# Layer-norm graph attention on one core: the last four batches' projections in plain float32, and another order for the end

## The chip, the core and the metric

The kernel runs on one core of a Trainium2 chip. The metric is the device time in microseconds. Before the change three runs took 1846.33, 1846.67 and 1848.8 us, so the median is 1846.67 us. One more run was taken with a profile; it took 1845.31 us, of which 1843.2 us lie between the first and the last instruction (the span). All times inside the kernel below come from that profiled execution.

The engines are named as in the profile: PE is the matrix engine (PEld its weight loads), DVE the vector engine, ACT the scalar engine, POOL the general engine, SP the engine that issues most DMAs.

## What is computed

The input `x` is 128 batches of 128 x 512 float32, `adj` one 128 x 128 matrix for all. Two layers, cut to what matters:

```python
# layer 0: W = adj, r = relu(rowmax(W @ x) + b)
x = layernorm(x + r)
# layer 1: masked attention with 8 heads of 64, then a projection, a norm, a residual
q, k, v = split(x @ w_qkv)                       # 512 -> 3 x 512
attn = softmax(where(adj == 0, -inf, q @ k.T / 8))
o = (attn @ v) @ w_proj + b_proj                 # 512 -> 512, the projection
o = o + layernorm(o) * gamma + beta
x = layernorm(x + o)
```

## The kernel before, in words

**Split products.** Every dense product (q, k, v and the projection) is made from a high part, a low part and a difference of each operand, in a float32 type that the matrix engine takes in a single pass (`fp32r` in the rows). `product` (L809) makes 8 matmuls of 128 x 512 into one bank of the accumulator memory and `product_d` (L816) makes 4 more into another. The two are joined when they are read. For the projection of batch b the left operand is made as follows after the attention product `AV` (L938): `omask` (L959) cuts off the low bits on DVE, `osub` (L962) makes the rest on DVE, `ohigh` (L965) scales the high part on ACT (on POOL for every fourth batch), and `od` (L968) subtracts on POOL. Then come `po` (8 matmuls), `pod` (4 matmuls), `pmain` (L1005, DVE: first bank plus bias) and `prest` (L1017, DVE: adds the second bank and sums the row). The three forms of `w_proj` are made once, at the start, and stay in place.

**Plain float32 products.** A matmul of plain float32 operands appears in the profile as two matmul records. The kernel before uses such products in five places: `conv` (L626), two v products at the very start (L773), the scores `S` (L847), `AV`, and the transposes.

**Stages of a batch.** Load, row maximum (`conv`, `cmax`), the first norm (`norm0`), a transpose of `x` by DMA (`xpl`, `xrow`, `xcross`), its split forms (`xmask`, `xsub`, `xhigh`, `xd`), the dense products of a group of four batches (`dm`, `dd`, read by `main` on ACT and `rest` on DVE), `S`, `masked`, `rmax`, `exps`, `recip`, `wts` (the softmax), the transpose of the weights by DMA (`pln`, `row`, `cross`), `AV`, the projection, and then the tail: `sq1`, `sm1`, `st1`, `n1a`, `n1b` (norm of o, scaled, and added to the residual), `sq2`, `sm2`, `st2`, `norm2` (the last norm), `out`. `res`, `resx`, `resb`, `reso` reload `x`, renew its norm, add beta, and add o; `resx`, `resb` run on POOL, `reso` on POOL for the first batch of the last group and on DVE for the other three.

The weights of the last group (batches 124 to 127) are transposed on PE (`T`, `wT`) and not by DMA.

**What sets the order.** A batch is b = 4g + i, in groups g of four, g = 0 to 31. Each step has a place: a planner's time in the tables `FIRST`, `STEADY`, `LAST`, plus 55.2952 for each group. `plan.sort` (L1149) sorts all steps by place and emits them in this order, so each engine runs its own instructions in the order of the places. Only the order counts; the numbers themselves are no times in the last two groups (`LAST[-2]` for 120 to 123, `LAST[-1]` for 124 to 127). `TWO` chooses the engine or form of single steps; `HOMES` says, for each kind of tile and each group, which of a few buffers it uses. A step whose buffer is still being read waits for that reader.

**What exists but is not used.** `plain`, `lp`, `ocopy` (L974 to L987), and the first branches of `po` and `pmain` are already in the code. `TWO["plain"]` is all zero and the tables have no `lp` or `ocopy`, so none of them is issued.

Of the kernel before, what the change touches and what calls it, by code (L numbers as in the profile page):

```python
# [8 lines left out]
FP = mybir.dt.float32  # L9
# [60 lines left out]
    'pmain': [83.702, 69.241, 100.828, 106.975],  # L70
# [13 lines left out]
    'norm2': [110.625, 102.524, 149.986, 131.962],  # L84
# [119 lines left out]
        'load': [-91.734, -89.477, -107.242, -114.634],  # L204
        'conv': [-79.525, -78.308, -102.395, -106.644],
        'cmax': [-78.282, -74.809, -97.173, -102.720],
        'relu': [-74.462, None, -95.620],
        'bn': [-84.588, -84.468],
        'ba': [-79.682, -83.743],
        'rstdx': [-78.667],  # L210
        'shiftx': [-73.931],
        'add0': [None, None, -94.016, -93.757],
        'sq0': [None, None, -92.245, -92.088],
        'rstd0': [None, None, -90.665],
        'shift0': [None, None, 1.956],
        'norm0': [-72.634, -70.162, -87.160, -65.629],
        'xpl': [-70.704, -62.494, -82.728, -52.644],
        'xrow': [-67.509, -55.672, -79.256, -47.934],
        'xcross': [-61.696, -54.959, -69.654, -44.141],
        'xmask': [-56.802, -49.006, -67.480, -38.547],  # L220
        'xsub': [-56.208, -47.336, -48.300, -38.074],
        'xhigh': [-56.405, -35.357, -48.848, -36.590],
        'xd': [-13.227, -33.711, -14.237, -9.757],
        'dm': [21.746, 35.982, 28.529, 24.986, -12.154, -20.919, -31.752, -22.843, -16.374, -23.208, 3.153, -23.262],
        'dd': [23.983, 44.501, 28.964, 43.094, -0.464, -0.154, -2.296, 3.849, 2.837, 6.978, 9.141, -3.429],
        'main': [25.819, 57.797, 40.607, 32.331, -7.607, -8.068, -28.601, -21.948, -7.441, -14.251, 7.551, -22.713],
        'rest': [26.194, 59.179, 55.083, 48.674, 1.465, 1.877, 5.828, 8.803, 4.926, 9.286, 9.980, -0.010],
        'S': [12.874, 24.637, 13.908, 27.284],
        'masked': [15.703, 26.864, 16.095, 31.214],
        'rmax': [15.733, 40.798, 24.980, 58.564],  # L230
        'exps': [19.267, 49.838, 29.967, 74.789],
        'recip': [20.091, 53.481, 40.286, 110.599],
        'wts': [21.502, 58.271, 41.826, 298.180],
        'pln': [29.804, 61.505, 44.952, 425.772],
        'row': [29.811, 62.249, 56.821, 855.336],
        'cross': [71.356, 71.129, 392.061, 855.704],
        'AV': [450.591, 228.845, 746.233, 898.316],
        'omask': [674.319, 308.605, 1366.729, 1365.220],
        'osub': [770.925, 364.572, 1435.526, 1878.235],
        'ohigh': [754.357, 413.868, 1441.862, 1849.429],  # L240
        'od': [988.972, 501.318, 1621.330, 2107.197],
        'po': [974.369, 651.327, 1588.162, 2528.823],
        'pod': [1064.642, 652.548, 1865.274, 2557.810],
        'pmain': [1435.941, 736.245, 1973.007, 2868.655],
        'prest': [1546.675, 797.306, 2173.489, 2884.326],
        'res': [74.125, 210.960, 1968.966, 1160.560],
        'resx': [666.741, 389.233, 2173.124, 1523.596],
        'resb': [1621.095, 663.168, 2352.412, 1829.810],
        'reso': [1640.878, 1001.671, 2395.120, 2960.734],
        'sq1': [1604.545, 997.678, 2512.030, 2977.847],  # L250
        'sm1': [1686.157, 999.741, 2175.055, 3079.791],
        'st1': [1828.719, 1108.345, 2545.132, 3018.165],
        'n1a': [1812.470, 1044.747, 2812.405, 3131.435],
        'n1b': [1850.820, 1165.266, 2862.346, 3159.644],
        'sq2': [2493.237, 1760.632, 2976.836, 3254.808],
        'sm2': [1921.825, 1828.948, 3018.160, 3473.653],
        'st2': [2528.768, 2033.360, 3135.653, 3542.995],
        'norm2': [2639.507, 2052.978, 3248.824, 3833.127],
        'out': [2968.875, 2348.409, 3425.425, 3981.636],
    },  # L260
    -1: {
        'load': [-74.411, -94.944, -121.973, -105.338],
        'conv': [-67.640, -67.401, -118.263, -97.835],
        'cmax': [-66.723, -65.650, -114.893, -95.280],
        'relu': [-58.744, None, -89.292],
        'bn': [-61.917, -72.350],
        'ba': [-60.526, -67.833],
        'rstdx': [-56.851],
        'shiftx': [-56.726],
        'add0': [None, None, -62.987, -77.999],  # L270
        'sq0': [None, None, -57.978, -56.682],
        'rstd0': [None, None, -53.335],
        'shift0': [None, None, -44.091],
        'norm0': [-51.929, -48.752, -41.363, -43.244],
        'xpl': [-47.768, -35.477, -40.163, -26.662],
        'xrow': [-47.424, -34.373, -36.605, -25.909],
        'xcross': [-44.093, -25.037, -30.491, -19.630],
        'xmask': [-35.420, -9.955, -16.920, -10.187],
        'xsub': [-25.027, -6.256, -12.316, -6.545],
        'xhigh': [-27.780, -5.984, -14.077, -6.723],  # L280
        'xd': [-3.120, 2.338, -1.405, 2.029],
        'dm': [313.202, 1288.056, 1009.352, 606.354, 5.041, -3.508, 3.931, -0.002, 5.901, 0.270, 3.338, 5.883],
        'dd': [1260.174, 1334.786, 1944.004, 2066.246, 15.556, 181.181, 16.195, 16.891, 14.449, 10.199, 16.353, 204.999],
        'main': [531.917, 1726.881, 2232.003, 1492.821, 19.146, 4.178, 12.068, 2.946, 20.970, 15.386, 13.588, 251.078],
        'rest': [1584.380, 2117.448, 2732.560, 2262.970, 213.729, 258.245, 214.247, 228.661, 100.506, 20.060, 216.387, 259.031],
        'S': [390.580, 829.031, 841.642, 913.116],
        'masked': [618.393, 1107.535, 1243.436],
        'rmax': [666.560, 1118.244, 1747.034, 1340.778],
        'exps': [953.376, 1201.075, 2054.184, 1674.549],
        'recip': [2062.103, 1344.889, 2203.646, 1765.129],  # L290
        'wts': [2152.417, 1549.500, 2396.365, 2203.399],
        'T': [2266.940, 1973.871, 2472.696, 2322.244],
        'wT': [2282.301, 2172.089, 2576.164, 2457.055],
        'AV': [2284.230, 2274.397, 2965.116, 2626.927],
        'omask': [2595.470, 2280.785, 3162.865, 2988.471],
        'osub': [2820.893, 2434.855, 3429.992, 3159.684],
        'ohigh': [2750.204, 2451.872, 3286.893, 3316.324],
        'od': [3039.224, 2892.794, 3633.889, 3616.193],
        'po': [3173.682, 2577.770, 3825.461, 3766.452],
        'pod': [3271.990, 2953.722, 3870.796, 3770.602],  # L300
        'pmain': [3468.211, 2900.856, 3911.014, 3861.021],
        'prest': [3666.752, 3079.656, 4140.759, 3904.577],
        'res': [2958.126, 2645.090, 3764.261, 3341.762],
        'resx': [3336.479, 2694.938, 3829.281, 3414.706],
        'resb': [3731.310, 3045.395, 4024.715, 4056.273],
        'reso': [3972.867, 3167.661, 4170.783, 4168.563],
        'sq1': [3766.697, 3103.563, 4364.182, 4151.003],
        'sm1': [3983.741, 3230.880, 4380.221, 4279.414],
        'st1': [3972.922, 3228.819, 4501.812, 4281.125],
        'n1a': [4089.474, 3272.042, 4496.099, 4397.115],  # L310
        'n1b': [4148.072, 3277.728, 4609.403, 4496.104],
        'sq2': [4242.312, 3322.068, 4711.667, 4682.169],
        'sm2': [4188.352, 3487.589, 4757.450, 4584.842],
        'st2': [4259.490, 3603.405, 4771.316, 4769.754],
        'norm2': [4307.713, 3762.541, 4852.913, 4776.119],
        'out': [4308.243, 3922.137, 4896.248, 4875.983],
    },
}
SETUP = {
    'adjT': -5368.795,  # L320
# [7 lines left out]
    'wl': [-2261.511, -2387.200, -2300.619, -2399.284, -3580.705, -3099.647, -2837.573, -3730.432, -3902.648, -3283.909, -2914.244, -4174.857, -1243.704, -7.632, 8.590, -809.145],  # L328
    'gamma': -2581.890,
    'gammb': -2280.655,  # L330
    'gammc': -3464.839,
}
TWO = {
    'plain': [0, 0, 0, 0],
    'bn': [1, 0],
    'd': [0, 1, 0, 1, 1, 1, 1, 1],
    'dense': [0, 1, 0, 0, 0, 0, 0, 0, 0, 0, 0, 0],
    'h': [0, 0, 0, 0, 1, 0, 0, 0],
    'po': [1, 0, 1, 0],
    'tail_mask': [0, 0, 0, 1],  # L340
# [144 lines left out]
def tile_adj_resnorm_d2(  # L485
# [12 lines left out]
    nc = tc.nc  # L498
    B, T, D = x.shape
    P = 128  # L500
# [678 lines left out]
```

## Time and profile before

| what | value |
|---|---|
| median of three runs | 1846.67 us |
| profiled execution, its own time | 1845.31 us |
| its span, first to last instruction | 1843.2 us |
| mean granted PE clock | 0.994 of full |
| end of the last matmul (`po`/`pod` of batch 126) | 1827.70 us |
| end of the last `norm2` (batch 126) | 1840.15 us |
| one matmul of 128 x 512 in the single-pass type, start to start in a stream | 0.227 us |

The profile's page has one row for each engine, a strip of 40 slices over the span, the DMA queues, and the costliest groups of instructions. Closer answers of the trace are used below: a table of stages (busy time of each engine between two times), a list of waits (who waited for whom), and a timeline (single instructions in order of time, with the idle time before them in brackets). A name such as `pm_('o', 127)` is the first bank of the projection of batch 127, `pd_` the second bank, `pp_` both in a double bank; `w_h`, `w_l`, `w_d` at the end are memory of the qkv weights that is used again for the split forms of batches 124 to 127.

### The profile page before, as it was taken

To read this page: it belongs to the slowest core of one execution; us is meant where nothing else is said; L and a number is where in the kernel's file an instruction comes from. 1 tells how busy PE (TensorE), PEld (TensorE's weight loads), DVE (VectorE), ACT (ScalarE), POOL (GpSimd) and SP (SyncE) were. 2 spreads that over 40 slices of the span, in tenths; PEclk is the share of its full clock that TensorE was granted. 3 is DMA by queue.
4 is the path that set the end of the run, shared out by engine and by line. 5 is a ranking of instruction groups with operands and counts; after the bars stand their busy time and mean duration, and the time that the engine had idled before them with its cause. 6 is when DMAs were issued, how large, how long until landed. Compare 5 with 4: busy or idle time off the path is not lost. (4 is left out here: it accounts for less than half of the span.)

```text
span 1843.2 us, 32644 instructions
## 1 busy us (share of the span) xinstructions
PE 1805.7 (98%) x10541; PEld 1426.9 (77%) x10541; DVE 1535.2 (83%) x2551; ACT 1556.9 (84%) x3958; POOL 1293.9 (70%) x1937
## 2 busy tenths in 40 slices
PE   7999999999999999999999999999999999999995
PEld 4778778787777788787788777778787877777773
DVE  7988888888887888888888888888888888889975
ACT  6898888888898888898888888888888888978864
POOL 4265667767677767667767677767677676678967
PEclk9999999999999999999999999999999999999997
DMA  5466765667665667766567656576757576756641
GB/s 161 141 160 176 182 163 164 162 161 187 170 176 156 168 156 200 172 163 168 157 171 198 174 155 166 156 183 182 176 154 169 161 187 171 182 146 172 158 112 57
DMA packets 486138, 302.89 MB, mean 164 GB/s; under 512 B 399440, under 2 KB 403664, under 8 KB 485968
## 3 DMA queue, kind: packets, MB, share of 16 engines
q1 hardware_dynamic: 485104, 299.70, 62.1%
q8 instruction: 83, 1.36, 0.3%
q10 hardware_dynamic: 864, 1.12, 0.2%
q14 instruction: 87, 0.71, 0.1%
HBM read 72.16 MB, written 131.07 MB: 110 GB/s over the span
## 5 line engine op out<-in xcount | busy, mean ns | idle before, releaser
L898 ACT ACTIVATE e<-e,nmax 128x128 f32<-128x128 f32 x1016 | 392.6, 392 | 5.3 <-DVE nmax L881 5.3
L745 POOL TENSOR_TENSOR od<-oh,ol 128x512 fp32r<-128x512 f32 x124 | 165.0, 1331 | 133.8 <-DVE ol L963 78.0
L913 ACT COPY planes<-e 128x2048 uint16<-128x2048 uint16 x124 | 234.4, 1890 | 4.5 <-issue 1.6
L1051 POOL TENSOR_TENSOR sum<-sum,mhalf 128x1 f32<-128x1 f32 (+1 forms) x287 | 213.6, 744 | 23.9
L1045 ACT ACTIVATE square<-o,sum 128x512 bf16<-128x512 f32 x256 | 184.1, 719 | 33.1 <-DVE o L1039 29.2
L1036 POOL TENSOR_TENSOR xb<-xb,o 128x512 f32<-128x512 f32 x125 | 163.4, 1307 | 53.4 <-DVE o L1039 50.8
L898 ACT ACTIVATION_READ_ACCUMULATOR e<-e,nmax 128x1 f32 x1016 | 194.2, 191 | 0.0
L873 DVE SCALAR_TENSOR_TENSOR e<-psc,mask 128x1024 f32<-128x1024 f32 x127 | 152.3, 1217 | 44.3 <-PE psc L859 41.7
L1032 POOL TENSOR_TENSOR xb<-xb,beta_sb 128x512 f32<-128x512 f32 x128 | 166.9, 1304 | 2.7
L907 DVE TENSOR_TENSOR e<-e,sums 128x1024 f32<-128x1024 f32 x128 | 161.4, 1261 | 1.1
L1066 DVE SCALAR_TENSOR_TENSOR o<-o,sum,gamma_sb 128x512 f32<-128x512 f32 x128 | 98.5, 769 | 71.4 <-POOL sum L1054 61.6
L881 DVE TENSOR_REDUCE nmax<-e 128x8 f32<-128x1024 f32 x127 | 152.6, 1202 | 1.1
L739 POOL TENSOR_SCALAR oh<-oxh 128x512 fp32r<-128x512 f32 x31 | 64.0, 2065 | 113.4 <-DVE oxh L735 27.3
L712 ACT COPY xplanes<-xt 128x1024 uint16<-128x1024 uint16 x124 | 129.2, 1042 | 13.8 <-DMA rowsx<-xplanes 11.8
L859 PEld LDWEIGHTS psc<-qkT 64*128 64x128 f32 x2048 | 119.6, 188 | 19.6 <-issue 17.9
L859 PE MATMUL psc<-qkT 64*128 64x128 f32 x2048 | 132.6, 279 | 0.6 <-DVE o L1039 0.6
L628 PE MATMUL pa<-xt,adjT 128*128 128x512 f32 x256 | 132.0, 600 | 0.5 <-DVE adjT L557 0.4
L1029 POOL TENSOR_SCALAR xb<-xb,sum 128x512 f32<-128x512 f32 x128 | 119.2, 931 | 17.6 <-DMA xb<-in_x_dram 17.4
L945 PE MATMUL pav<-eT,v 128*64 128x128 f32 x2048 | 127.5, 276 | 1.8 <-DVE e L873 0.9
L945 PEld LDWEIGHTS pav<-eT,v 128*64 128x64 f32 x2048 | 110.4, 137 | 19.5 <-issue 10.3
L1039 DVE SCALAR_TENSOR_TENSOR o<-o,sum,xb 128x512 f32<-128x512 f32 x128 | 100.6, 787 | 20.8 <-POOL sum L1051 15.5
L1087 ACT ACTIVATE o<-o,sum 128x512 f32<-128x512 f32 x128 | 103.2, 807 | 12.3 <-POOL sum L1083 12.2
(4286 smaller groups left out, 5529.9 us busy)
## 6 DMA issues: line engine op xcount, KB each, us to landing
rows<-planes SPq DMA_DIRECT2D x124, 512.0 KB, 3.1
xt<-in_x_dram SPq DMA_DIRECT2D x128, 256.0 KB, 3.1
xb<-in_x_dram SPq DMA_DIRECT2D x128, 256.0 KB, 2.9
out_dram<-o SPq DMA_DIRECT2D x128, 256.0 KB, 3.0
rowsx<-xplanes SPq DMA_DIRECT2D x124, 256.0 KB, 2.5
wraw<-in_L_gnn_w_qkv_dram SPq DMA_DIRECT2D x8, 256.0 KB, 3.4
xT<-rowsx SPq DMA_TRANSPOSE x124, 3.8
eT<-rows SPq DMA_TRANSPOSE x124, 5.0
```

Source lines behind the costliest of these rows:

```text
L745: engine.tensor_tensor(d, h.bitcast(FP), l.bitcast(FP), op=ALU.subtract)
L859: nc.tensor.matmul(psc[:, s, hp, :], qkT[hs, hp, i, :], qkT[hs, KC + hp, i, :], start=not with_mask, stop=not with_mask or hp == HP - 1,)
L873: nc.vector.scalar_tensor_tensor(es[b], pscs.pop(b).rearrange("p s a m -> p (s a) m"), scale, mask_b, op0=ALU.mult, op1=ALU.add,)
L881: nc.vector.tensor_reduce(nmaxs[b], es[b], AX.X, ALU.max, negate=True)
L898: nc.scalar.activation(es[b][:, j, :], src[:, j, :], AF.Exp, bias=nmax[:, j : j + 1], scale=by, accum_out=sums[b][:, j : j + 1],)
L907: nc.vector.tensor_tensor(es[b], es[b], sums.pop(b)[:, :, None].to_broadcast([P, H, P]), op=ALU.mult,)
L913: nc.scalar.copy(pl, es.pop(b).rearrange("p h m -> p (h m)").bitcast(U16).rearrange("p (m s) -> p s m", s=2),)
L945: nc.tensor.matmul(pavs[b][s * HD : (s + 1) * HD, hp, :], v[:, h * HD : (h + 1) * HD], eT[:, s * HP + hp, :], start=True, stop=True,)
L1032: nc.gpsimd.tensor_tensor(xbs[b], xbs[b], beta_sb, op=ALU.add)
L1036: engine.tensor_tensor(xbs[b], xbs[b], os[b], op=ALU.add)
L1045: nc.scalar.activation(square, src, AF.Square, bias=s[:, 0:1], scale=-float(D), accum_out=s[:, 1:2],)
L1051: nc.gpsimd.tensor_tensor(s, s, mhalf[:, :n], op=ALU.pow)
```

## The change

For batches 124 to 127 the projection is no longer split. The attention result is copied once from the accumulator memory (`ocopy`, ACT), multiplied with the unsplit `w_proj` by four plain float32 matmuls into a single bank (`po`), and read once with bias and row sum (`pmain`). `omask`, `osub`, `ohigh`, `od`, `pod` and `prest` are gone for these four batches. `w_proj` is loaded a second time in four pieces of 128 rows (256 KB each) by `lp` on the SP queue, into the q part of the last group's q and k (`praw`), which is free once all four `S` of that group have read it. All places of the last two groups, and the buffers (`HOMES`) of the last three or so groups, are replaced. `FIRST`, `STEADY` and `SETUP` stay, but for two changes of 0.001.

```diff
 TWO = {
-    'plain': [0, 0, 0, 0],
+    'plain': [1, 1, 1, 1],
...
+    def praw(n):
+        return qkTs[NG - 1][:, n].rearrange("p g t -> p (g t)")
+
     def lp(b):
         n = b % G
-        nc.sync.dma_start(
-            w_d[:, :, D + n * P : D + (n + 1) * P].bitcast(FP),
-            w_proj[:, n * P : (n + 1) * P].rearrange("(c p) f -> p c f", p=P),
-        )
+        nc.sync.dma_start(praw(n), w_proj[n * P : (n + 1) * P, :])
 
     def ocopy(b):
-        n = b % G
-        oraws[b] = w_d[:, :, n * P : (n + 1) * P].bitcast(FP)
+        oraws[b] = tile_at(work, "xh", [P, KC, P], FP, f"oxh_{b}", "oxh", *divmod(b, G))
         nc.scalar.copy(oraws[b], pavs.pop(b))
...
             pom, r = bank(("o", b), 0, False), oraws.pop(b)
             for kc in range(KC):
                 nc.tensor.matmul(
-                    pom, r[:, kc, :], w_d[:, kc, D : 2 * D].bitcast(FP), start=(kc == 0), stop=(kc == KC - 1),
+                    pom, r[:, kc, :], praw(kc), start=(kc == 0), stop=(kc == KC - 1),
                 )
```

Of the table of the last group (`LAST[-1]`), the rows that the text speaks of:

```diff
-        'S': [390.580, 829.031, 841.642, 913.116],
+        'S': [568.110, 411.072, 408.806, 560.824],
-        'AV': [2284.230, 2274.397, 2965.116, 2626.927],
-        'omask': [2595.470, 2280.785, 3162.865, 2988.471],
-        'osub': [2820.893, 2434.855, 3429.992, 3159.684],
-        'ohigh': [2750.204, 2451.872, 3286.893, 3316.324],
-        'od': [3039.224, 2892.794, 3633.889, 3616.193],
-        'po': [3173.682, 2577.770, 3825.461, 3766.452],
-        'pod': [3271.990, 2953.722, 3870.796, 3770.602],
-        'pmain': [3468.211, 2900.856, 3911.014, 3861.021],
-        'prest': [3666.752, 3079.656, 4140.759, 3904.577],
+        'AV': [2877.033, 2419.907, 3106.656, 2910.722],
+        'lp': [1372.781, 1579.539, 775.912, 1383.693],
+        'ocopy': [2944.230, 2625.101, 3364.788, 3210.244],
+        'po': [3112.878, 2645.586, 3631.628, 3427.698],
+        'pmain': [3309.789, 2821.443, 3713.225, 3475.853],
```

Sorted by place, the new tables give these orders at the end (number = batch; `dm31.0` is product 0 of group 31):

```text
PE   ... S127 S124 dd31.3 dm31.1 po120 pod120 dm31.2 dm31.0 dd31.1 dm31.3 AV123 po122 dd31.2 dd31.0
     pod122 po123 T125 T127 pod123 AV125 T124 po125 T126 AV124 AV127 AV126 po124 po127 po126
ACT  ... norm2121 exps124 norm2120 sq1122 wT125 sq1123 ocopy125 wT124 sq2122 wT127 sq1125 wT126 ocopy124
     sq2123 norm2122 sq2125 ocopy127 norm2123 sq1124 ocopy126 norm2125 sq1127 sq1126 sq2124 sq2126 sq2127
     norm2124 norm2126 norm2127
DVE  ... pmain123 prest123 n1a122 rest31.0 n1b122 pmain125 reso125 n1a123 n1b123 n1a125 n1b125 pmain124
     pmain127 n1a124 pmain126 reso126 n1b124 n1a126 reso127 n1b126 n1a127 n1b127
POOL ... resx123 od123 reso122 st1122 resb123 sm1122 resb125 reso123 st1123 sm2122 st2122 sm1123 st1125
     sm1125 resx124 sm2123 st2123 sm2125 resx127 resx126 resb124 st2125 reso124 resb126 sm1124 resb127
     st1127 sm1127 st1124 sm1126 st1126 sm2124 st2124 sm2126 st2126 sm2127 st2127
SP   ... cross120 row123 lp126 cross123 res122 lp124 lp127 lp125 res125 res123 res127 out121 res126 res124
     out120 out122 out123 out125 out124 out126 out127
```

The old tables give, for PE, `... T125 dd31.3 T124 AV125 AV124 T127 T126 po123 pod123 po125 AV127 pod125 AV126 po124 pod124 po127 pod127 po126 pod126`; and for SP `... cross122 row123 cross123 res123 res122 out121 res125 out120 res124 res127 ...`.

## The prediction

> **What bounds the kernel now.** I read the page first: the rows of the engines and the strip of slices.
>
> ```profile
> PE 1805.7 (98%) x10541; PEld 1426.9 (77%) x10541; DVE 1535.2 (83%) x2551; ACT 1556.9 (84%) x3958; POOL 1293.9 (70%) x1937
> ...
> PE   7999999999999999999999999999999999999995
> ...
> PEclk9999999999999999999999999999999999999997
> ```
>
> PE is busy everywhere but in the last slice, where its clock falls too. The body is PE-bound and its tables stay. So only the end can move, and there I asked for stages: the last dense products, the stretch from the first long idle of PE to its last matmul (1827.70), and what follows.
>
> ```profile
> core 0: us, PE busy (x) PEld busy (x) DVE busy (x) ACT busy (x) POOL busy (x), PEclk, DMA share, GB/s
> 1640.00:1741.29 101.29, 99.71 (x610) 79.38 (x609) 88.35 (x145) 84.72 (x206) 82.30 (x117) 1.00 0.68 179
> 1741.29:1811.64 70.35, 68.78 (x445) 54.44 (x443) 56.71 (x87) 47.11 (x146) 54.97 (x70) 1.00 0.34 95
> 1811.64:1827.70 16.06, 9.65 (x25) 6.73 (x24) 7.22 (x15) 6.62 (x15) 15.08 (x26) 0.68 0.20 65
> 1827.70:1843.20 15.50, 0.00 (x0) 0.00 (x0) 7.01 (x14) 5.59 (x11) 8.06 (x19) 0.59 0.14 51
> ```
>
> Up to 1811.64 PE hardly idles. Then POOL is busy 15.08 of 16.06 us, PE only 9.65, at a clock of 0.68; then come 15.5 us without a matmul. The list of waits from 1811 on, and the timeline of PE, name the causes:
>
> ```profile
> DVE o L1013 <- DMA out_dram<-o: 4.5, 1, 4.5
> ...
> PE pm_('o', 127)_20094 L813 <- ACT w_h L741: 3.9, 1, 3.9
> ...
> PE pd_('o', 127)_20104 L819 <- POOL w_d L745: 2.5, 1, 2.5
> ```
> ```profile
> 1816.45 0.39 PE L814 MATMUL pm_('o', 127)_20094<-p_l,w_l 128*128 128x512 f32 x1
> ...
> 1822.77 0.63 PE L813 MATMUL pp_('o', 126)_20110<-p_h,w_h 128*128 128x512 f32 x1
> 1823.20 0.63 PE L814 MATMUL pp_('o', 126)_20110<-p_l,w_l 128*128 128x512 f32 x1
> ```
>
> PE waits for `ohigh` and `od` of batch 127, that is for the splitting, and its last 16 or so matmuls start 0.43 us apart where they started 0.227 apart.
>
> **The change, part by part.**
>
> *Removed.* Per batch: `omask`, `osub` and `prest` on DVE (0.68 + 0.68 + 0.69, with prest's row sum moved into pmain), `od` on POOL (1.28), `ohigh` on ACT (0.62) or, once, on POOL (1.84), and 12 matmuls (12 x 0.227 = 2.72 us). For four batches: DVE 8.2 us, POOL 4 x 1.28 + 1.84 = 7.0 us, ACT 3 x 0.62 = 1.9 us.
>
> *Added on ACT.* Four `ocopy`, 4 x 0.57 (the copy of the same shape from the accumulator memory at L776 took 0.574 us): 2.3 us against 1.9 removed. Nothing, as a sum.
>
> *Added on PE.* Four plain float32 matmuls per batch. The nearest row is L773, the same shape and count:
>
> ```profile
> 18.32 3.60 PE L773 MATMUL pv<-wraw,xraw 128*128 128x512 f32 x8
> ```
>
> The next instruction started at 21.75, so 3.43 us at full clock. The mask products of batch 127 (L853) took 1.92 us for two, that is 3.84 for four. I take 3.5, nearer to the row of equal form; ends 3.4 and 3.85. PE gets 4 x (3.5 - 2.72) = 3.1 us more work (2.8 to 4.5).
>
> *PE's end.* From 1741.29 to 1827.70 PE took 86.4 us. Idle in it: 3.9 + 2.5 in the waits above, and 0.9 + 0.5 + 0.2 for `T` and `AV` before: 8.0 us. Slow clock: 8 matmuls of 127 took 2.76 (1.82 at full rate), its next four 1.87 (0.91), the 12 of 126 4.93 (2.72): 4.1 us. Dense and at full clock the old work would end at 1827.7 - 8.0 - 4.1 = 1815.6, with the new products at 1818.7.
>
> *What idle comes back.* I laid the new PE order backwards from 1818.7 with these rows (product 1.82, second product 0.91, AV 1.03, S 1.0, T 0.93, plain projection 3.5) and put the orders of ACT, DVE and POOL beside it with their rows. It gives these late points. `AV123` uses the bank that `main` of product 31.2 frees on ACT: 0.4 us. `ocopy125` stands on ACT behind `sq1123`, which needs `prest123`: `po125` 0.9 us late. `od123` now stands on POOL behind `resx123`, whose reload waits for the buffer of batch 120 (`n1b120`, about 1791.3), then 2.9 us of DMA, 0.77 and 1.28: about 1796.5, against 1797.5 for `pod123`; no idle, 1 us of slack. `ocopy124`, `ocopy127`, `ocopy126` end at about 1808.8, 1812.8, 1815, each ahead of its product, which now runs behind 3.5 us of another. I take 2.0 us of idle (0 to 5): PE ends at 1820.7.
>
> *The clock, row and rule.* The row: PE idled 3.92 us from 1811.73, ran on at full rate for about 1.2 us, then at half. Read alone, it could be the thin work of that stretch, and the new end would run its last two products at half rate as well: 2 x 3.5 = 7.0 us more. [...] my idle points, all under 1 us, keep the clock full; so do 0.9 us of idle at 1717.5 in this trace, with 1.00 around it. [...]
>
> *After the last matmul.* Before: 12.45 us to the end of the last `norm2` (1827.70 to 1840.15), because 127 and 126 ended together and shared the chain, and then 3.05 us for the output. New: `po127` ends 3.5 us ahead of `po126`. From `po126` the DVE order sets the end: `pmain126` 0.8, then reso126, n1b124, n1a126, reso127, n1b126, n1a127, n1b127 at 0.67 to 0.75: 5.1 us; then sq2127 0.9, sm2 and st2 1.1, norm2127 0.9: 8.8 us.
>
> *POOL, row and rule.* POOL is what could stretch this: from `st1122` to `st1124` it has 20.6 us of work in about 23 (its order with resb and reso at 1.28, resx 0.77, st1 0.85, st2 1.1, sm 0.2), without contention. `n1b` took 0.74 us at 1776.50, where POOL was idle, and 1.76 at 1788.50, beside a `resb`:
>
> ```profile
> 1788.43 1.28 POOL L1032 TENSOR_TENSOR xb<-xb,beta_sb 128x512 f32<-128x512 f32 x1
> ...
> 1788.50 1.76 DVE L1039 SCALAR_TENSOR_TENSOR o<-o,sum,xb 128x512 f32<-128x512 f32 x1
> ```
>
> [...] By the plain rows, nothing. POOL has waits of its own (2 us before st1125) that take part of it; I add 1.5: 10.3 us after the last matmul.
>
> *Sum.* 1820.7 + 10.3 + 3.05 = 1834.05 against a span of 1843.2: -9.15 us. The profiled run becomes 1845.31 - 9.15 = 1836.2. It was 1.4 us below the median; from the median, 1846.67 - 9.15 = 1837.5 us.
>
> *Added on SP.* Four `lp` of 256 KB. Loads of this size land in 2.9 us; they go out by about 1784 and are needed at 1801. DMA is at 0.34 of its share in that stretch, so nothing by themselves. But `lp126` waits for `S124`, the last reader of the q part, at about 1776.6; queued behind it are cross123, res122, the other three lp, res125, res123. `cross123` went out at 1769.06 before; now at about 1777.5, landing 4.4 us later at 1782, for `AV123` at 1788: hidden by 6 us of PE work. `res122` waits for n1b121 (1781.6) anyway.
>
> *Buffers.* The 4.5 us wait of `pmain127` for an output's DMA was a reused o buffer. In the new plan 126 follows 125, whose output lands at about 1818 (needed at 1820); 127 follows 123 (1815.5, needed at 1816.2). No cost, thin slack. The other moved places (loads, first norms, reloads) lie beside a PE that is full, at no cost as long as it stays so; 0 to 1.5 us either way.
>
> **Rivals.**
>
> *The clock falls again.* [...] `po127` loses 2.3 and `po126` 3.5: with the gap 9.3 us, 1846.8, no change. For: it is what happens now. Against: POOL and DVE lose the 15 us that made the waits.
>
> *POOL becomes the bound.* The tail waits for resb127 and st1124 in full and the last matmuls idle some: 3 to 6 us, 1840.5 to 1843.5.
>
> *Slower: `lp126` blocks SP.* If `S124` is late, `cross123` and with it `AV123` and all of PE behind it stop. Past 6 us of lateness each us costs one; [...] the clock costs some 7 more. To eat the gain and 0.2% (9.2 + 3.7) `S124` must be about 12 us late, and the time then passes 1850. Against: its bank is freed by `masked125`, at about 1772, 4 us early.
>
> **How the numbers follow.** 0.2% (3.7 us) is about what a measurement of this kernel can tell from no change. The sum as it stands, give or take: 0.70 (1833.5 to 1841). POOL-bound 0.13. Clock falls 0.11. Slower 0.06. The range reaches from a PE without idle and no contention, 1834.0, less 1 us for the moved places, to the POOL case: 1833 to 1843. Faster by over 0.2% (below 1843.0): 0.83; within: 0.11; slower: 0.06.
>
> **What would show it.** Right: PE without a wait over 1.5 us up to its last matmul at 1819 to 1823; PEclk 1.00 there; 32 float32 records in the four projections, 3.4 to 3.85 us per batch; 10 us or so from the last matmul to the last norm2. Wrong: PE waiting for `ocopy` or `pod123`'s left operand, records 0.85 us apart at the end, `pmain` waiting for an output, or `AV123` waiting for a DMA.

## The result, and the profile after

The changed kernel takes 1839.68 us (median of five runs, 1837.87 to 1842.82) against 1846.67 us before: a ratio of 0.9961, 95% interval 0.9949 to 0.9973, or 7.0 us less. It ran once more beside the first experiments: 0.9958 (0.9946 to 0.9971). The forecast was 1837.5.

The profiled execution of the changed kernel took 1842.82 us (span 1841.0), the longest of its five. Lines of its code are 4 or 5 lower than before (`od` L741, `ocopy` L982, the plain `po` L991, `pmain` L1004, `resb` L1027, `n1b` L1034, `n1a` L1061). It was already 5.2 us behind the kernel before where both still run the same instructions: the first matmul of batch 93's projection starts at 1390.52 us, before at 1385.33. So all stages below are counted from that matmul, and the time from it to the end of the span is called the **stretch**: 457.87 us before, 450.48 after, 7.4 less; in the second profile of the changed kernel 449.85, 8.0 less.

The stages at the end of the changed kernel:

```profile
core 0: us, PE busy (x) PEld busy (x) DVE busy (x) ACT busy (x) POOL busy (x), PEclk, DMA share, GB/s
1646.60:1747.00 100.40, 99.12 (x607) 79.57 (x608) 85.58 (x143) 85.27 (x219) 78.68 (x116) 1.00 0.63 166
1747.00:1818.00 71.00, 68.56 (x435) 52.49 (x434) 56.16 (x88) 51.43 (x143) 56.87 (x79) 1.00 0.43 130
1818.00:1827.11 9.11, 9.11 (x22) 3.74 (x20) 2.44 (x7) 4.92 (x10) 8.62 (x15) 1.00 0.23 86
1827.11:1841.00 13.89, 0.00 (x0) 0.00 (x0) 6.21 (x13) 5.48 (x11) 8.89 (x21) 0.59 0.15 57
```

From 1818 us on PE works without a gap up to its last matmul. Over the 16.06 us that end with this matmul it is busy for 15.27 us at a clock of 1.00, where before it was busy for 9.65 at 0.68; POOL is busy for 14.98 of them, before for 15.08. The last matmul ends at 1827.11, 436.59 us behind the matmul of batch 93 (before 442.37): 5.8 us earlier. After it come 13.89 us instead of 15.5. The timeline of PE shows the four plain projections:

```profile
1808.04 3.70 PE L991 MATMUL pm_('o', 125)_19971<-qkT,oxh 128*128 128x512 f32 x8
...
1816.54 3.70 PE L991 MATMUL pm_('o', 124)_20038<-qkT,oxh 128*128 128x512 f32 x8
1820.08 3.60 PE L991 MATMUL pm_('o', 127)_20063<-qkT,oxh 128*128 128x512 f32 x8
1823.51 3.60 PE L991 MATMUL pm_('o', 126)_20078<-qkT,oxh 128*128 128x512 f32 x8
```

Each has 8 records for 4 matmuls, and from start to start 3.43 to 3.54 us. What the table of stages can't say is which engine holds the end back. The chain that ended last does; here is its part from 1818 us on (start, length, what):

```profile
1818.23 0.20 POOL sum L1045
...
1819.52 1.50 POOL xb L1024 x2
1821.02 1.24 POOL xb L1027
...
1823.47 1.23 POOL xb L1031
1824.70 1.23 POOL xb L1027
1825.92 0.20 POOL sum L1049
1826.12 1.22 POOL xb L1027
...
1829.64 0.58 POOL sum L1046
1830.25 0.06 DVE o L1034
```

It runs on POOL from 1813.0 to 1830.3, and from 1800 us on it does not pass through PE at all. PE's last matmul ends beside it, in the shadow. For the kernel before, the same view reaches back only to 1831.63 us, so what bound its end has to come from the experiments.

### The profile page after: what moved, and what is told of

Same layout as the page of the kernel before. It is cut to its first block, busy times and chain, and to the rows that moved or that the text cites. A ratio compares the mean times of both kernels' runs of the same rounds, so it can differ in the third digit from the quotient of the medians.

```text
span 1841.0 us, 32606 instructions
## 1 busy us (share of the span) xinstructions
PE 1808.0 (98%) x10525; PEld 1422.8 (77%) x10525; DVE 1527.8 (83%) x2539; ACT 1557.0 (85%) x3959; POOL 1287.5 (70%) x1932
## 4 chain that ended last, share of the span: by engine, by line
PE 86%; POOL 5%; DVE 4%; ACT 2%; issue 2%; DMA 1%; SPq 0%; POOLq 0%; DVEq 0%; ACTq 0%
PE psc L855 6%; PE pav L941 6%; PE pa L624 5%; POOL sum L1046 1%; DVE o L1034 1%; POOL xb L1027 1%; POOL xb L1031 1%; DVE nmax L877 0%; DVE e L869 0%; POOL xb L1024 0%; DVE o L1061 0%; PE pv L769 0%; POOL sum L1045 0%; ACT e L894 0%; POOL od L741 0%
## 5 line engine op out<-in xcount | busy, mean ns | idle before, releaser
L741 POOL TENSOR_TENSOR od<-oh,ol 128x512 fp32r<-128x512 f32 x124 | 164.6, 1328 | 139.4 <-DVE ol L959 77.5
L1046 POOL TENSOR_TENSOR sum<-sum,mhalf 128x1 f32<-128x1 f32 (+1 forms) x287 | 218.2, 760 | 23.9
L1027 POOL TENSOR_TENSOR xb<-xb,beta_sb 128x512 f32<-128x512 f32 x128 | 165.7, 1294 | 2.9
L1061 DVE SCALAR_TENSOR_TENSOR o<-o,sum,gamma_sb 128x512 f32<-128x512 f32 x128 | 103.9, 812 | 69.2 <-POOL sum L1049 65.7
L708 ACT COPY xplanes<-xt 128x1024 uint16<-128x1024 uint16 x124 | 129.2, 1042 | 12.5 <-DMA rowsx<-xplanes 10.3
L1024 POOL TENSOR_SCALAR xb<-xb,sum 128x512 f32<-128x512 f32 x128 | 111.1, 868 | 12.2 <-DMA xb<-in_x_dram 12.1
L1034 DVE SCALAR_TENSOR_TENSOR o<-o,sum,xb 128x512 f32<-128x512 f32 x128 | 98.5, 769 | 24.0 <-POOL sum L1046 19.1
L696 ACT ACTIVATE xt<-xt,sum 128x512 f32<-128x512 f32 x128 | 103.3, 809 | 11.9 <-POOL sum L690 11.9
```

Of the source, the lines that this page charges most:

```text
L741: engine.tensor_tensor(d, h.bitcast(FP), l.bitcast(FP), op=ALU.subtract)
L1027: nc.gpsimd.tensor_tensor(xbs[b], xbs[b], beta_sb, op=ALU.add)
L1046: nc.gpsimd.tensor_tensor(s, s, mhalf[:, :n], op=ALU.pow)
```

## The experiments

The ratio is to the kernel before on the same chip. The kernels ran on several chips, so rows are compared by the ratio and not by the median. The last three columns are of the profiled execution: the stretch, its part up to the end of the last matmul, and the rest. Counted from the matmul of batch 93, all fourteen profiles agree within 0.5 us up to batch 108.

| kernel | median us | ratio (95%) | stretch | to last matmul | rest |
|---|---|---|---|---|---|
| before | 1846.67 | | 457.87 | 442.37 | 15.50 |
| after | 1839.68 | 0.9961 (0.9949 to 0.9973) | 450.48 | 436.59 | 13.89 |
| after, again | 1838.88 | 0.9958 (0.9946 to 0.9971) | 449.85 | 435.93 | 13.92 |
| new order, split form | 1856.37 | 1.0057 (1.0044 to 1.0069) | 466.67 | 447.57 | 19.10 |
| old order, plain form, loads first | 1844.87 | 0.9990 (0.9982 to 0.9998) | 455.08 | 437.84 | 17.24 |
| old order, plain form, loads later | 1841.34 | 0.9970 (0.9959 to 0.9981) | 451.41 | 434.15 | 17.26 |
| before, PE's gaps filled | 1846.15 | 1.0000 (0.9992 to 1.0008) | 456.96 | 439.35 | 17.61 |
| after, half of the plain products | 1839.18 | 0.9961 (0.9947 to 0.9974) | 450.33 | 433.42 | 16.91 |
| after, ballast on POOL | 1845.30 | 0.9991 (0.9984 to 0.9997) | 455.87 | 439.54 | 16.33 |
| after, POOL relieved, early reloads | 1839.18 | 0.9961 (0.9949 to 0.9974) | 451.47 | 439.26 | 12.21 |
| the same, tail in another order | 1841.92 | 0.9975 (0.9966 to 0.9984) | 451.76 | 438.19 | 13.57 |
| after, POOL relieved, tail only | 1838.93 | 0.9953 (0.9939 to 0.9966) | 450.44 | 438.27 | 12.17 |
| after, warm start | 1837.48 | 0.9946 (0.9933 to 0.9958) | 448.86 | 434.93 | 13.93 |
| POOL relieved and warm start | 1837.13 | 0.9945 (0.9933 to 0.9958) | 448.78 | 436.53 | 12.25 |

**The changed kernel again.** No edit.

> The changed kernel once more, on the same chip as its neighbours here. In its first profile it ran 5.2 us behind the kernel before at batch 93, in code that the change does not touch: PE came to full clock only at 13.7 us, against 7.8. If that lag is chance, this profile shows another lag at batch 93, while the stretch from the first product of batch 93 to the end stays within 1 us of 450.4 us (458.0 in the kernel before). If the lag belongs to the change, it is again near 5 us. Time: 1836 to 1842 us.

Its batch 93 starts at 1387.25 us, 3.3 us earlier than in the first profile, and its stretch is the same within 0.6. The lag of the first profile belongs to that execution and not to the change.

**The new order alone.** The changed kernel with the split form given back to the last group:

```diff
-    'plain': [1, 1, 1, 1],
+    'plain': [0, 0, 0, 0],
+L['omask'] = [u + 1 for u in L['AV']]
+L['osub'] = [u - 0.5 for u in copies]
+L['ohigh'] = copies
...
+L['pod'] = [u + 0.2 for u in L['po']]
+L['prest'] = [u + 0.2 for u in L['pmain']]
```

> The new order of the end with the projection of 124 to 127 in split form again (omask, osub, ohigh, od, pod, prest put beside the places of ocopy, po and pmain; no second load of the weights). Theory: the form yields the gain, since PE's 6.4 us of waits and the 4.1 us at half clock come from the splitting. Then this loses 6 to 12 us against the changed kernel: 1844 to 1851, with PE waiting for a left operand near the end. Rival, the order yields it: within 2 us of the changed kernel.

It is slower than the kernel before by 0.57%, and its stretch is some 16 us longer than that of the changed kernel, more than the 6 to 12 us expected. PE waits 6.3 us for `ohigh` of batch 127, and its clock falls to a mean of 0.81 behind 1807.9. From the list of waits (who waits for whom: us in all, times, longest):

```profile
PE pm_('o', 127)_20090 L824 <- ACT w_h L752: 6.3, 1, 6.3
POOL w_h L750 <- DVE oxh L746: 4.4, 1, 4.4
POOL w_d L756 <- ACT w_h L752: 4.2, 2, 2.2
```

The new order needs the short path from `AV` to `po`; by itself it gains nothing. I placed the split steps by hand, so this says that the order doesn't carry the gain, not that no order for the split form could.

**The plain form alone.** The old order with the plain products, the four loads first ahead of the reloads `res123` and `res122` on SP, then, in a second kernel, behind them:

```diff
 TWO['plain'] = [1, 1, 1, 1]
-L['lp'] = [960.0, 961.0, 962.0, 963.0]
+L['lp'] = [1914.0, 1915.0, 1916.0, 1917.0]
```

> The old order with plain float32 projections for 124 to 127 (ocopy at the places of ohigh, the four loads of the weights on SP behind the transpose of batch 123, pmain where it was). Theory: the form yields the gain; the stretch from batch 93 to the end falls from 458.0 to 449 to 453 us, the time to 1838 to 1842. Rival, the order yields it: the stretch stays within 2 us of 458.0, the time within 2 us of 1846.7.

> The old order with plain products, as in the run before, but the four loads of w_proj stand on SP behind the reloads res123 and res122 instead of ahead of them. Nothing else differs. Theory (the loads blocked SP: they waited for the last score product, the reloads queued behind them came late, and POOL waited 9.9 us for them, so that a norm and then rest31.1 and a transpose on PE were late): POOL's wait for the reload falls to some 4 us as in the kernel before, PE has no wait over 1 us in the end, its clock stays full, and the time is 2 to 3 us lower, 1842 to 1843. Rival (the old order costs those 2 us anyway, whatever SP does): the time stays within 0.7 us of 1844.9, and PE waits for the same or another link.

The place of the loads alone is worth 0.9990 against 0.9970, some 3.7 us (2 to 3 expected). The first of the two kernels misses its expectation for that: a stretch of 455.08 us, not 449 to 453. SP's queue and POOL with the loads first:

```profile
1782.70 1.77 SPq L992 DMA_DIRECT2D qkT<-in_L_gnn_w_proj_dram  x4
1784.56 11.76 SPq L1035 DMA_DIRECT2D xb<-in_x_dram  x2
```
```profile
1789.20 0.77 POOL L1038 TENSOR_SCALAR xb<-xb,sum 128x512 f32<-128x512 f32 x1 [9.90 <-DMA xb<-in_x_dram]
```

and with the loads later:

```profile
1777.63 13.36 SPq L1035 DMA_DIRECT2D xb<-in_x_dram  x2
1791.08 1.81 SPq L992 DMA_DIRECT2D qkT<-in_L_gnn_w_proj_dram  x4
```
```profile
1780.52 0.77 POOL L1038 TENSOR_SCALAR xb<-xb,sum 128x512 f32<-128x512 f32 x1 [4.00 <-DMA xb<-in_x_dram]
```

The loads wait for the last `S` (1782.7), and what is queued behind them waits too. POOL stands 9.9 us for the reload instead of 4.0. Further down the same chain PE waits 2.5 us for a transpose's input with the loads first (0.5 with them later), and its clock is at 0.50 for the 3.4 us behind that. With the loads well placed, the plain form in the old order gives a stretch 6.5 us shorter than before: most of the gain.

**PE's gaps filled.** The kernel before with 14 and 7 matmuls into a free bank, in the two gaps of 3.9 and 2.5 us; nothing reads them.

```diff
+    at(u31 + 3740.0, fill, 14)
+    at(u31 + 3768.0, fill, 7)
```

> The kernel before with 14 more matmuls of 128 x 512 between the projections of 124 and 127 (3.2 us in an idle of 3.9) and 7 more (1.6 us in 2.5) ahead of the second product of 127; nobody reads their result. If idle of PE is what halves the clock, the clock stays full, the last 16 matmuls start 0.227 us apart and the stretch falls by 2.5 to 4 us, to 454 to 455.5. If the clock falls for another reason, it stays 458 +- 0.7.

The clock stays at 1.00 to the last matmul, which comes 3.0 us earlier, but the stretch falls by 0.9 us only (to 456.96; 454 to 455.5 expected) and the time does not change: the rest grows from 15.5 to 17.6. On DVE the steps behind the last matmul are `pmain126` (L1013) and then `n1a124` (L1066). In the kernel before:

```profile
1827.79 0.69 DVE L1013 SCALAR_TENSOR_TENSOR o<-pp_('o', 126)_20110,bias_sb 128x512 f32<-128x512 f32 x1 [3.65 <-issue]
1828.40 1.04 DVE L1066 SCALAR_TENSOR_TENSOR o<-o,sum,gamma_sb 128x512 f32<-128x512 f32 x1
```

and with the gaps filled:

```profile
1825.48 0.69 DVE L1013 SCALAR_TENSOR_TENSOR o<-pp_('o', 126)_20133,bias_sb 128x512 f32<-128x512 f32 x1 [0.77 <-issue]
1827.05 1.74 DVE L1066 SCALAR_TENSOR_TENSOR o<-o,sum,gamma_sb 128x512 f32<-128x512 f32 x1 [0.88 <-POOL sum L1054]
```

Before, `pmain126` starts 0.09 us after the last matmul has ended, so PE's end did lie on the path. But when it comes earlier, `n1a124` waits for POOL, and then takes 1.74 us instead of 1.04 beside a `resb` on POOL. So POOL stood less than 1 us behind PE, and bringing PE's end forward was worth no more than that even before the change.

**Half of the plain products.** The changed kernel with two of the four matmuls in each of the four projections: half of each sum is left out, and with it 7 us of PE.

```diff
-            for kc in range(KC):
+            for kc in range(KC // 2):
```

> The changed kernel with only two of the four plain matmuls in each of the four projections; the other half of each sum is left out. PE has 4 x 1.75 = 7 us less work at the end. Theory of the prediction (PE's end sets the tail: projections, then a fixed chain of some 11 us): the last matmul comes 5 to 7 us earlier and the time is 4 to 6 us lower, 1833.5 to 1835.5. Rival (the tail is bound by POOL and DVE, whose work for batches 123 to 126 is the same): the last matmul comes earlier, but the stretch after it grows by nearly as much, and the time is at most 1.5 us lower, 1838 or more.

Nothing is gained. The last matmul comes only 2.5 to 3.2 us earlier, since PE now waits for ACT (1.8 us for the `wT` of an `AV`, with its clock at 0.50 from 1810.26 to 1813.67 behind it, and 0.65 us for `ocopy126`), and the rest grows by 3.0. The chain is that of the changed kernel, on the same rows of POOL:

```profile
1819.53 1.22 POOL xb L1031
1820.75 1.22 POOL xb L1027
1821.97 0.20 POOL sum L1049
1822.16 1.22 POOL xb L1027
```

**Ballast on POOL.** The changed kernel with one useless subtraction on POOL behind each `ocopy`:

```diff
+        nc.gpsimd.tensor_tensor(w_d[:, :, n * P : (n + 1) * P], beta, beta, op=ALU.subtract)
```

> The changed kernel with four useless subtractions of 128 x 512 float32 on POOL, one behind each of the four copies of the attention result, into the memory that the removed od wrote. Nothing reads them. This gives POOL back 4 x 1.28 = 5.1 us of the 7.0 us that the change took from it, and gives no other engine anything. Theory (POOL's queue from about 1802 to 1830 sets the end, and it is the lightening of POOL that the change gains by): the time rises by 4 to 5.5 us, to 1843.5 to 1845. Rival (PE's end sets the tail, as the prediction had it): at most 1.5 us more, 1841 or less.

```profile
1809.79 1.49 POOL L987 TENSOR_TENSOR w_d<-beta_sb 128x512 fp32r<-128x512 f32 x1
...
1812.93 1.49 POOL L987 TENSOR_TENSOR w_d<-beta_sb 128x512 fp32r<-128x512 f32 x1
...
1820.42 1.03 POOL L987 TENSOR_TENSOR w_d<-beta_sb 128x512 fp32r<-128x512 f32 x1
...
1822.81 1.04 POOL L987 TENSOR_TENSOR w_d<-beta_sb 128x512 fp32r<-128x512 f32 x1
```

By the ratios these 5.05 us of POOL cost 5.5 to 6.1 us, by the two profiles of the changed kernel 5.4 to 6.0 us of the stretch. Of the latter, 1.0 to 1.8 us arise before the first of them (see below), so the subtractions themselves account for 4.3 us. PE's last matmul comes 3.0 us later as well, since PE now waits 1.8 us for `ocopy127`, but the chain that ended last stays on POOL from 1806.6 to 1834.5 us. The ballast takes most of the gain away with no other engine's work touched.

**POOL relieved, and the tail's order.** The changed kernel with `resb` of 126 and 127 and `reso` of 124 on DVE, and three reloads and their norms early; then a tail in which 124 and 127 end first:

```diff
+L['res'][0], L['res'][3], L['res'][2] = 18.1, 18.2, 18.3
+TWO['tail_vector'] = [1, 1, 1, 1]
+        engine = nc.vector if b >= B - 2 else nc.gpsimd
```

> The changed kernel, with work taken from POOL at the end: the reloads of 124, 127 and 126 go out early, their resx and resb(124) run in POOL's idle time before, and resb(126), resb(127) and reso(124) run on DVE. About 5.4 us of work leave POOL's last 20 us, 2.0 us come to DVE. Theory (POOL's queue[...] are what makes the stretch after the last matmul 13.9 instead of the 10.3 us that I summed): that stretch falls to 11 to 12 us and the time by 2 to 3 us, to about 1836.5. Rival (the chain itself, DVE's eight steps in a row and the last statistics, is what is long): within 1 us of the changed kernel, 1838.5 to 1840.

> As the kernel with POOL relieved, and beside it the tail's steps are put in an order in which batches 124 and 127 finish their second norm before the last projection, 126, ends, so that only 126's own chain follows the last matmul. Walked through with the durations of the trace, the chain of 126 alone takes some 10 us after the last matmul, against 13.9 now. Theory (three chains interleaved on DVE, ACT and POOL make the tail long): 3.5 to 4.5 us lower than the changed kernel, about 1835.5. Rival (each step of one chain waits for another engine, so a single chain is no shorter than the three interleaved): within 1.5 us of the relieved kernel, on either side.

The rest shrinks from 13.9 to 12.2 us, nearly as expected, but PE's end comes 2.7 us later, and the time does not fall. The early reloads are the cause: an `AV` now waits from 1771 to 1773 for its transposed weights, and the clock halves for 3.4 us behind that.

```profile
PE pav L948 <- DMA eT<-rows: 2.1, 1, 2.1
```
```profile
1765.00:1774.00 9.00, 6.88 (x73) 5.69 (x73) 6.60 (x8) 2.63 (x3) 7.39 (x8) 1.00 0.78 251
1774.00:1777.30 3.30, 3.30 (x15) 2.35 (x12) 1.04 (x2) 0.00 (x0) 1.51 (x1) 0.50 0.15 61
```

The other order has a median 2.7 us higher; the intervals overlap a little, but its fastest run (1840.77) is slower than the slowest of the other (1840.64). Its stretch is only 0.3 us longer, though: in the profiles most of the difference arises before batch 93 (1388.34 us against 1386.43), where the two kernels do the same, so I can't put it down to the tail. What failed is the gain of 3.5 to 4.5 us that I had expected: `norm2124` on ACT waits 3.5 us for POOL's statistics, and `sq1126`, which starts the last batch's chain, stands behind it. In taking three interleaved chains apart I had put a waiting step in front of the one that mattered.

**POOL relieved, tail only.** The same three steps on DVE, without the early reloads:

```diff
+L['resb'][3], L['resb'][2] = 3480.0, 3712.0
+L['sm1'][0], L['reso'][0], L['n1a'][0] = 3574.0, 3575.0, 3580.0
```

> The changed kernel with resb(126), resb(127) and reso(124) on DVE instead of POOL and sm1(124), n1a(124) a little earlier, and without the early reloads of the first POOL experiment, which had put 2.1 us of waiting for a DMA and one half-rate window on PE at 1772. POOL loses 3 x 1.23 = 3.7 us behind 1823, DVE gets 3 x 0.69 = 2.1 us. Theory (POOL bound): PE's last matmul stays 436 us behind the first of batch 93's projection, the stretch after it falls from 13.9 to about 12.2, and the time by 1.5 to 2.5 us, to 1836.5 to 1838. Rival (DVE's chain, made longer, takes the place of POOL's): within 0.7 us of the changed kernel, 1839 to 1840.5.

The rest is 12.17, as expected, but the last matmul comes 1.7 us later, and neither the stretch nor the time falls as it should have. Of these 1.7, 1.2 arise between 1748 and 1763 us, where the instructions and their order are still those of the changed kernel (PE waits 0.7 us for ACT to read out product 31.6's bank). The ballast kernel and the last kernel below show the same 1.2 us, the other variants of the changed kernel don't; I did not find why. Now the chain does pass through PE:

```profile
1816.33 3.63 PE pm_('o', 124)_20038 L996 x8
1819.96 3.43 PE pm_('o', 127)_20063 L996 x8
1823.39 3.45 PE pm_('o', 126)_20080 L996 x8
```

By the times (0.9953 against 0.9961 and 0.9958, intervals over one another) the relief is not told from nothing.

**Warm start.** Six bfloat16 matmuls on zeros ahead of PE's first input, alone and with the relieved tail:

```diff
+        nc.gpsimd.memset(square, 0.0)
+        for _ in range(6):
+            nc.tensor.matmul(t[:, 0, :], square[:, :P], square, start=True, stop=True)
```

> The changed kernel with six bfloat16 matmuls on zeros ahead of everything on PE, in the 4.3 us in which PE waits for its first input. The eleven profiles so far show PE's clock at half until 7.8 to 9.7 us in most, and until 13.7 to 14.2 us in three, among them the profiled run of the changed kernel, which was the slowest of its five. Theory (the start of the clock explains the spread of the runs: [...]): full clock by 8.2 us at the latest, no run over 1841, the median 0.5 to 2 us lower, 1837 to 1839. Rival (the spread comes from elsewhere, DMA for example): the median within 0.5 us and runs over 1841 as before.

> The relieved tail (resb(126), resb(127), reso(124) on DVE) and the six early matmuls together, as the version that the runs so far point to. If both act and add: 1835.5 to 1837.5. If neither acts: 1839 to 1840.

The first products of the row maximum show the clock. In the changed kernel:

```profile
5.11 3.78 PE L624 MATMUL pa<-xt,adjT 128*128 128x512 f32 x4 [0.38 <-DVE adjT L553]
...
11.04 3.19 PE L624 MATMUL pa<-xt,adjT 128*128 128x512 f32 x4
```

and in the last kernel:

```profile
4.86 1.98 PE L629 MATMUL pa<-xt,adjT 128*128 128x512 f32 x4 [0.39 <-DVE adjT L558]
...
9.43 1.88 PE L629 MATMUL pa<-xt,adjT 128*128 128x512 f32 x4
```

The same four records take 3.8 us ahead of the changed kernel's first clock record (13.66 us), half clock by their length, and 1.9 at full. In the kernel with the warm start alone they took 2.75 and then 3.25: the clock rose early, and fell again over a gap of 2.1 us. By the ratios the two kernels (1837.48 and 1837.13 us) are 2.2 to 3.0 us below the changed kernel, with no run over 1838.82; their intervals (0.9933 to 0.9958) overlap its own (0.9949 to 0.9973, 0.9946 to 0.9971), so a small gain is likely and not settled. Nor do the profiles put it at the start: with the warm start alone, batch 93 starts at 1387.04 us against 1387.25 in the second profile of the changed kernel. The stretch is 1.0 to 1.6 us shorter, and that arises between batches 109 and 111, where the early matmuls change nothing; the last kernel shows the same, and I did not find why. So the clock as the cause is not shown. These two are the fastest versions that I ran, 0.54% below the kernel before, and not told apart.

## Why the prediction was right, and where its reasons were not

The sign and the size held: -9.15 forecast, -7.0 measured, 2.2 us beside the forecast and inside the range. The mechanism behind it did not hold in one main step. That the sum came out near the mark is in part luck: I had PE's end come 7.0 us earlier for PE's own reasons, and POOL happens to lose 7.0 us of work.

- **Plain projection, 3.5 us each**: 3.43 to 3.54. `ocopy`, 0.57 taken: 0.562 to 0.591. Right.
- **PE's end, -7.0 forecast** (1827.7 to 1820.7): -5.8 and -6.4. The idle points that I had listed (`AV123` 0.4, `po125` 0.9) did not show; in their place PE waited 1.3 us for the double bank of product 31.1, freed by `masked124`, and 0.3 and 0.5 us for the last two `wT`. I had no row for that wait: the buffers of the last groups are all new, and I had laid out the orders, not each bank.
- **The clock**: 1.00 up to the last matmul, against the row read alone. That idle under 1 us keeps it full was an estimate, from the one point of 0.9 us at 1717.5 in the kernel before. The filled gaps show it from the other side: the old order's end with no idle over 1.6 us ran at full clock (1.00 from 1811.64 to 1825.39). Only the idle that matters is shorter than the 3.9 us of the kernel before: 2.1 and 2.5 us were enough (last section).
- **"Dense and at full clock the old work would end at 1815.6" as the measure of the gain**: this is the step that failed. I took 12.1 us of idle and slow clock on PE as time that the change gives back, and let a chain of fixed length follow the last matmul. Filling the gaps brought PE's end 3.0 us forward, the stretch 0.9 and the time nowhere; taking 7 us of PE's work from the changed kernel did nothing either. POOL, busy for 15.08 of 16.06 us in my own table of stages, was the bound within 1 us, and stayed it after the change. That PE's gaps were its symptom is argued and not run: one of the two was a wait for POOL (2.5 us), the other for ACT (3.9 us), which had itself waited for DVE and POOL.
- **After the last matmul, 10.3 us to the last `norm2`**: 10.9 (1827.11 to 1838.04), then 2.96 for the output. I had charged POOL 1.5 us, an estimate from two `n1b` (0.74 us, and 1.76 beside a `resb`). Between `st1122` and the end of `st1124` POOL was busy for 22.4 of 23.9 us; I had estimated 20.6 of 23. `n1a124` took 1.73 us beside a `resb` (an `n1a` at 1830.92, with only 128 x 1 statistics on POOL, 0.75), and waited 1.7 us for `sm1124` before that.
- **What the gain is, then**: POOL loses 7.0 us (four `od` and one `ohigh`), and 5.05 us given back cost 4.3 by the profile, 5.5 to 6.1 by the ratios. At that rate 7.0 us of POOL are worth 6 to 8.5 us; 7.0 were measured. (The removal of `od` alone, with the rest of the split form in place, was not run, and DVE lost 8.2 us as well; what these may add is not told apart.) PE's projections fit into the shadow, but only just: with POOL relieved by 3.7 us the chain moves to them and the time hardly falls, so the two bounds lie about 1 us apart.
- **"POOL becomes the bound"**, held at 0.13, named the right mechanism (the tail waits for `resb127` and `st1124` in full) at a price of 3 to 6 us that was too high; the cost against my sum was 2.
- **`lp126` on SP**: the load went out at 1781.63, 1776.4 if the lag of 5.2 us is taken off (1776.6 forecast); `cross123` at 1782.06, and `AV123` at 1795.53 did not wait. The rival's mechanism is real, as the old order showed (3.7 us for four loads in front of the reloads), and in the new order it has a cover. That order with the load behind `cross123` was not tried.
- **The o buffers**: no `pmain` waited for an output. Right.

The plain form in the old order yields 6.5 us of the stretch, both together 7.4 to 8.0, so by the profiles the new order adds 1 to 1.5. By the times that is not settled (0.9970 against 0.9961 and 0.9958, intervals over one another). Without the plain form it costs 8.8.

## What to carry to other kernels

When PE idles near the end, look for who makes it idle before adding up its idle time. Here that was POOL, busy for 94% of the stage. The busy share alone does not settle it: in the changed kernel PE is as busy as POOL, and work taken from PE still counts for nothing. Two kernels settle it cheaply: take away half of the suspected work, and add ballast of known length to the rival. Here each microsecond put on POOL cost about one; taking more off it than the change did hardly paid, because PE's end stood right behind. Four loads that had to wait for their buffer held back the two reloads queued behind them on SP, at a cost of 3.7 us; place such a load behind what is urgent.

## What I had not expected of the hardware

- Of the twelve executions without early matmuls, seven come to full clock (the first clock record of the trace) at 7.8 to 9.7 us and five at 13.1 to 14.2, with the same instructions. The kernel before is among the seven (7.81) and the first profile of the changed one among the five (13.66). Why the times differ was not shown. At batch 93 the five were 2.7 us behind the seven in the mean, a good third of what the change is worth; that the clock is the cause was not tested by itself.
- A statistic of 128 x 1 on POOL (`sum<-sum,mhalf`) takes 0.57 us in the quiet and up to 1.53 us in the busy part near the end of the changed kernel (at 1753.76). Small steps on POOL were not cheap here: the mean of the 256 of this shape was 0.76 us.
- The length of a gap does not decide alone whether PE's clock falls. Gaps of 2.1 us (the `AV` above; the warm start) and 2.5 us (the transpose, loads first) each brought 3.4 us at half clock, but the same 2.1 us in the last kernel did not; of two waits of 1.8 us, the one with half of the products brought it and the one with the ballast did not. In the fourteen traces every stretch between two changes of the clock lasts a whole multiple of 3.41 us (1809.06, 10.24 and 3.41 us in the kernel before: 530, 3 and 1 times). Cut into windows of that length, PE was busy for at most 1.74 us of the window before each fall, and for at least 1.53 us of each window behind which the clock stayed full. In the kernel before it was busy for 1.22 us from 1813.46 to 1816.87, where the clock fell, and for 1.68 us of the window ahead of that, behind which the clock stayed at 1.00. So a window about half idle was enough here. That the same gap of 2.1 us had two outcomes may come from where it lies in such a window; this was not tested by itself.
